# The middle column of a binary depthwise convolution taken from TensorE to DVE and ACT, and the input turned in later slices

## The chip, the cores and the metric

The kernel runs on one core of one Trainium2 chip. The metric is the device time of one execution in microseconds; the time before is the median of three runs.

## The reference

The input x has 16 images of 56 x 56 pixels and 384 channels, float32. Two layers follow each other, each added to its input:

```
x = x + attention(gn(x))       # dilated 3 x 3 attention, three groups of 128 channels, dilations 1, 2, 3
x = x + conv(gn(x), sign(w))   # depthwise 3 x 3 convolution, taps are -1, 0 or 1, zero padding
```

`gn` takes mean and variance over 12 channels and all pixels of an image and gives (g - m) / sqrt(s + eps), so for each image and channel it is a scale and a bias. In the second layer every channel has nine taps of its own. Of these, the taps with kx = 1 (the middle kernel column: the pixel above, the pixel itself, the pixel below) are what the change moves.

## The kernel before

The work is cut into 112 chunks: 16 images of 7 chunks, each of 8 rows (448 pixels). Channels lie on the partitions, in three groups of 128. The program is planned by hand in slices: a piece of work is put into a slice and an order within it with `at(when, order, piece)`, a chunk starts every 9 slices (`STEP`), and the pieces are emitted in the order of the slices. The framework then orders the instructions of each engine; each engine works its own queue in that order.

`plan_a` loads a chunk of x and turns it (TensorE transposes into PSUM, ACT copies to `xa`, DVE takes `bn_stats`, and SP's queue stores it channel-major as `xd`). In the kernel before the three groups are turned in slices 0, 2 and 4 of the chunk, for all images but the first. `plan_b` is the attention: products for q, k and v on TensorE (L464), scores as products q x k on DVE (L517) summed on TensorE (`ps`, L502), the softmax, then for each of nine groups of three neighbours the weights are spread over the partitions by TensorE into `pb_a` (L581), multiplied by v on DVE (`w`, L588) and added on GpSimd (L596); at last the output projection `po` (L614), its residual add on DVE (L617) and the store of the layer's result as `x1d`.

`plan_c` is the convolution. For channel groups 0 and 1, `load` brings x1 with the three rows of taps on 96 partitions (3 x 32 channels, one copy a kernel row) into `z`; `normalise` applies scale and bias on ACT (L698); `convolve` multiplies by diagonal weights `kdiag` on TensorE, four sets of 32 channels side by side, three kernel columns into one PSUM tile `pc` (L712); DVE adds the layer's input `x1` (L719). The third group (`zg`, `taps_g`, `sum_g`) is done by ACT and GpSimd without TensorE. `turn` transposes the result back and stores it. For the last image, whose convolution can only run after all other work, `z_last`, `taps_last` on DVE and other buffers are used.

PSUM tiles of many kinds (`pkv`, `po`, `pt_x`, `pt_o`, `pt_s`, `pc`) share the pool `ps_mt` with three banks; `pq` has one buffer, `pb_a` one.

Of the kernel before, what the change touches and what calls it, by code (L numbers as in the profile page):

```python
# [17 lines left out]
P = 128  # L18
# [17 lines left out]
def dilated_attention_then_binary_conv(  # L36
# [99 lines left out]

    spread = const.tile([P, 2, P], BF16, name="spread")

    ktap = const.tile([P, NTAP], F32, name="ktap")

    kdiag = const.tile([K3, 3, JG * NQ, HD], F32, name="kdiag")

    xin_p = ctx.enter_context(tc.tile_pool(name="xin_p", bufs=1))
    z_p = ctx.enter_context(tc.tile_pool(name="z_p", bufs=2))
    xa_p = ctx.enter_context(tc.tile_pool(name="xa_p", bufs=3))
    st_p = ctx.enter_context(tc.tile_pool(name="st_p", bufs=2))
    dr_p = ctx.enter_context(tc.tile_pool(name="dr_p", bufs=3, space=DRAM))
    xn_p = ctx.enter_context(tc.tile_pool(name="xn_p", bufs=3))
# [6 lines left out]
    x1_p = ctx.enter_context(tc.tile_pool(name="x1_p", bufs=2))  # L155
    xg_p = ctx.enter_context(tc.tile_pool(name="xg_p", bufs=2))
    m_p = ctx.enter_context(tc.tile_pool(name="m_p", bufs=3))
    o_p = ctx.enter_context(tc.tile_pool(name="o_p", bufs=2))


# [34 lines left out]
    def load_small_weights():  # L195

        raw["small"] = t = m_p.tile([P, 3, PX], F32, tag="m", name="small")
        flat = t.rearrange("p k n -> p (k n)")
        at_ = [0]

        def room(parts, n):
            at_[0] += n
            return flat[:parts, at_[0] - n : at_[0]]

        raw["b"] = room(NG, P)
        raw["k"], raw["kp"] = room(K3, 3 * NG * NQ), room(K3, 3 * NG * NQ)
        raw["kg"] = room(P, NTAP)
# [4 lines left out]
        nc.sync.dma_start(raw["kg"], w_conv.rearrange("y x c m -> c (y x m)")[JG * P : (JG + 1) * P, :])  # L212

    def load_taps(ky, kx):
        k_in = raw["k"].rearrange("p (k s) -> p k s", k=3)
# [17 lines left out]
    def small_weights():  # L233
        pt = ps_mt.tile([P, 512], F32, tag="mt", name="pt_b")
        nc.tensor.transpose(pt[:, :NG], raw["b"], ident[:NG, :NG])
        nc.vector.tensor_copy(bias, pt[:, :NG])

        spread_f = raw["spread"].rearrange("r (f n) -> r f n", f=2)
        nc.gpsimd.memset(spread_f, 0.0)
        for rg in range(4):  # L240
            for f in range(2):
                for t in range(TERMS):
                    halves = spread_f[:, f].rearrange("r (h d) -> r h d", h=HEADS)
                    nc.gpsimd.affine_select(
                        out=halves, in_=halves, compare_op=ALU.not_equal, fill=1.0,
                        base=-(32 * rg + (2 * t + f) * HEADS),
                        pattern=[[-1, HEADS], [0, HD]], channel_multiplier=1,
                    )
# [12 lines left out]

        binary(raw["kp"], raw["k"])
        kp = raw["kp"].rearrange("p (k s) -> p k s", k=3)
        binary(ktap, raw["kg"])
# [7 lines left out]
        for kx in range(3):  # L272
            nc.vector.tensor_tensor(
                kdiag[:, kx],
                kp[:, kx, : JG * NQ].unsqueeze(2).to_broadcast([K3, JG * NQ, HD]),
                eye3.unsqueeze(1).to_broadcast([K3, JG * NQ, HD]),
                ALU.mult,
            )
        raw.clear()

    def rows(ap):
        return ap.rearrange("p (r w) -> p r w", w=W)
# [113 lines left out]
    stats0, stats1 = {}, {}  # L396
    xd, x1d = {}, {}
    mr0, mr1 = {}, {}
    first = {}
    last_term = {}  # L400

    def plan_a(m, t0):
# [36 lines left out]
            elif j == NG - 1:  # L439
                nc.scalar.dma_start(chunk_of(xd[b], c), first[c])  # L440

        at(t0 - 3 if b else FIRST + 2 * max(c - 2, 0), LOADS, load)
        for j in range(NG):
            at(t0 + 2 * j if b else FIRST + 2 * c + 1, STAGE_A, lambda j=j: turn(j))

    def plan_b(m, t0):

# [197 lines left out]
        for j in range(NG):  # L645
            at(t0 + 24 + j, PROJECT, lambda j=j: out_project(j))

    def plan_c(m, t0):

        b, c = divmod(m, NCH)  # L650
# [38 lines left out]
        def normalise(j):  # L689
# [9 lines left out]
            for edge in edges(j):  # L699
                nc.gpsimd.memset(edge, 0.0)  # L700

        def load_x():
            had["x1"] = x1 = x1_p.tile([P, JG, PX], F32, tag="x1", name="x1")
            nc.sync.dma_start(x1, chunk_of(x1d[b], c)[:, :JG])  # L704

        def convolve(j):
            pc = ps_mt.tile([P, 512], F32, tag="mt", name="pc")
            pcr = rows(pc[:, :PX])

            def tap(kx, q):  # L710
                lo, hi = max(0, 1 - kx), W - max(0, kx - 1)
                return nc.tensor.matmul(  # L712
                    pcr[q * HD : (q + 1) * HD, :, lo:hi], kdiag[:, kx, j * NQ + q, :],
                    rows(set_of(j, q))[:, :, lo + kx - 1 : hi + kx - 1], start=(kx == 1), stop=(kx == 2),
                )
# [3 lines left out]
            nc.vector.tensor_tensor(x1[:, j], pc[:, :PX], x1[:, j], ALU.add)  # L719

        lo, hi = (0 if c else 1), ROWS + (2 if c < NCH - 1 else 1)
        zp = zg[m % 2]

        def load_g():
# [21 lines left out]
        def taps_last(ky):  # L746

            mid = had["xg"][:, 1 : ROWS + 1, :]
            if ky == 0:
                had["m"] = m_p.tile([P, 3, PX], F32, tag="m", name="m")  # L750
            acc = rows(had["m"][:, 0])
            for kx in range(3):
                o = 3 * ky + kx
                nc.vector.scalar_tensor_tensor(  # L754
                    mid if o == 8 else acc, zp[:, ky : ky + ROWS, kx : kx + W], ktap[:, o : o + 1],
                    acc if o else mid, op0=ALU.mult, op1=ALU.add,
                )

# [7 lines left out]
        def taps_g(ky):  # L766
            t = m_p.tile([P, 3, PX], F32, tag="m", name="m")
            for kx in range(3):
                o = 3 * ky + kx
                nc.scalar.activation(  # L770
                    rows(t[:, kx]), zp[:, ky : ky + ROWS, kx : kx + W], AF.Copy, scale=ktap[:, o : o + 1]
                )
            if ky == 0:
                had["m"] = t
# [13 lines left out]
        def turn(s):  # L788
            pt = ps_mt.tile([P, 512], F32, tag="mt", name="pt_o")
            mid = had["xg"][:, 1 : ROWS + 1, :].rearrange("p r w -> p (r w)")  # L790
            for j in range(NG):
                src = mid if j == JG else had["x1"][:, j]
                nc.tensor.transpose(pt[:SUB, j * P : (j + 1) * P], src[:, s * SUB : (s + 1) * SUB], ident)  # L793
            if b < B - 1:
                osb = o_p.tile([SUB, C], F32, tag="osb", name="osb")
# [7 lines left out]
        if b == B - 1:  # L803
# [54 lines left out]
    def statistics(when, sets):  # L858
# [60 lines left out]
```

## Time and profile before

| | before |
|---|---|
| median of 3 runs | 5223.8 us (5223.65 to 5231.6) |
| the profiled execution's own time | 5223.35 us |
| its span | 5221.6 us |
| PE busy | 5085.7 us |
| DVE busy | 4199.0 us |
| POOL busy | 4242.2 us |
| ACT busy | 2310.7 us |
| mean DMA rate | 158 GB/s |
| mean granted TensorE clock | 0.984 |

The busy times are those of one profiled execution, the span is from its first to its last instruction. PE is TensorE's matmul, PEld its weight load, DVE VectorE, ACT ScalarE, POOL GpSimd, SP the engine whose queue issues most of the DMAs. A share of busy time is a mean over stages with different limits.

### The profile page before, as it was taken

To read this page: it belongs to the slowest core of one execution; us is meant where nothing else is said; L and a number is where in the kernel's file an instruction comes from. 1 tells how busy PE (TensorE), PEld (TensorE's weight loads), DVE (VectorE), ACT (ScalarE), POOL (GpSimd) and SP (SyncE) were. 2 spreads that over 40 slices of the span, in tenths; PEclk is the share of its full clock that TensorE was granted. 3 is DMA by queue.
4 is the path that set the end of the run, shared out by engine and by line. 5 is a ranking of instruction groups with operands and counts; after the bars stand their busy time and mean duration, and the time that the engine had idled before them with its cause. 6 is when DMAs were issued, how large, how long until landed. Compare 5 with 4: busy or idle time off the path is not lost. (4 is left out here: it accounts for less than half of the span.)

```text
span 5221.6 us, 75614 instructions
## 1 busy us (share of the span) xinstructions
PE 5085.7 (97%) x26885; PEld 2322.5 (44%) x26885; DVE 4199.0 (80%) x4125; ACT 2310.7 (44%) x4077; POOL 4242.2 (81%) x2950
## 2 busy tenths in 40 slices
PE   8999999999999999999999999999999999999976
PEld 4444444444444444444444444444444444444433
DVE  4898888888888888888888888888888888878764
ACT  3223444444444544444444444444445444444444
POOL 2677878888888888889888888888888888888881
PEclk8999999999999999999999999999999999999987
DMA  6444656666566565656666565665666656554445
GB/s 197 127 124 119 167 160 166 163 166 167 162 169 165 161 163 159 168 158 166 166 166 165 163 166 162 165 163 160 164 163 171 167 163 168 141 138 135 121 135 158
DMA packets 811631, 825.62 MB, mean 158 GB/s; under 512 B 360307, under 2 KB 801014, under 8 KB 811254
## 3 DMA queue, kind: packets, MB, share of 16 engines
q1 hardware_dynamic: 803270, 808.79, 56.9%
q10 hardware_dynamic: 7984, 12.00, 0.7%
q8 instruction: 213, 3.49, 0.3%
q14 instruction: 164, 1.34, 0.1%
HBM read 466.41 MB, written 231.21 MB: 134 GB/s over the span
## 5 line engine op out<-in xcount | busy, mean ns | idle before, releaser
L596 POOL TENSOR_TENSOR w<-w 128x1344 f32<-128x1344 f32 x672 | 2048.7, 3049 | 327.3 <-DVE w L588 279.1
L517 DVE TENSOR_TENSOR t<-pq,k 128x1344 f32<-128x1344 f32 x1008 | 1528.6, 1550 | 237.8 <-PE pq L464 236.6
L588 DVE TENSOR_TENSOR w<-pb_a,v 128x1344 f32<-128x1344 f32 x1008 | 1560.3, 1548 | 172.6 <-PE pb_a L581 91.9
L464 PE MATMUL pkv<-xn,wqkvT 128*128 128x448 f32 x3924 | 1542.2, 542 | 3.9 <-ACT xa L435 3.5
L464 PEld LDWEIGHTS pkv<-xn,wqkvT 128*128 128x128 f32 x3924 | 725.9, 190 | 664.7 <-issue 634.7
L614 PE MATMUL po<-y,wprojT 128*128 128x448 f32 x2016 | 834.9, 550 | 17.3 <-POOL y L600 17.3
L464 PE MATMUL pq<-xn,wqkvT 128*128 128x448 f32 x1962 | 834.9, 560 | 0.0
L698 ACT ACTIVATE z<-z,mrz 96x448 f32<-96x448 f32 x840 | 573.9, 751 | 266.0 <-DMA z<-x1d 239.7
L777 POOL TENSOR_TENSOR m<-m 128x1344 f32<-128x1344 f32 x210 | 639.1, 3044 | 43.3 <-ACT m L770 37.9
L502 PE MATMUL ps<-t,sel 128*32 128x448 f32 x6048 | 660.8, 546 | 0.3 <-DVE t L517 0.2
L474 ACT COPY v<-pkv 128x448 f32<-128x448 f32 x336 | 178.1, 530 | 918.3 <-PE pkv L464 911.1
L770 ACT ACTIVATE m<-zg,ktap 128x448 f32<-128x448 f32 x945 | 552.6, 658 | 15.1 <-POOL m L777 5.7
L614 PEld LDWEIGHTS po<-y,wprojT 128*128 128x128 f32 x2016 | 376.1, 191 | 374.1 <-issue 347.1
L712 PE MATMUL pc<-z,kdiag 96*32 96x440 f32 (+1 forms) x5040 | 519.3, 545 | 7.1 <-POOL z L700 4.3
L464 PEld LDWEIGHTS pq<-xn,wqkvT 128*128 128x128 f32 x1962 | 345.2, 190 | 318.8 <-issue 318.8
L617 DVE SCALAR_TENSOR_TENSOR xr<-po,bias,xr 128x448 f32<-128x448 f32 x336 | 227.9, 678 | 277.8 <-PE po L614 272.7
L435 ACT COPY xa<-pt_x 128x448 f32<-128x448 f32 x315 | 167.4, 534 | 618.2 <-PE pt_x L423 618.2
L558 POOL TENSOR_TENSOR rest<-ew,e 112x512 f32<-112x512 f32 x112 | 130.1, 1162 | 358.9 <-ACT e L554 358.9
L581 PE MATMUL pb_a<-aT,spread 24*128 24x448 bf16 x3024 | 369.5, 360 | 42.7 <-DVE w L588 36.7
L600 POOL TENSOR_TENSOR y<-y,w 128x448 f32<-128x448 f32 x336 | 381.7, 1136 | 23.8
L599 POOL TENSOR_TENSOR y<-w 128x448 f32<-128x448 f32 x336 | 382.8, 1139 | 19.3
L581 PEld LDWEIGHTS <-spread 24*128 24x128 bf16 x3024 | 100.8, 91 | 621.4 <-issue 603.6
(132 smaller groups left out, 4307.6 us busy)
## 6 DMA issues: line engine op xcount, KB each, us to landing
z<-x1d SPq DMA_DIRECT2D x570, 224.0 KB, 4.0
xr<-xd SPq DMA_DIRECT2D x112, 672.0 KB, 4.3
x1d<-xr SPq DMA_DIRECT2D x112, 672.0 KB, 3.2
xn<-xd SPq DMA_DIRECT2D x109, 672.0 KB, 4.5
xin<-in_x_dram SPq DMA_DIRECT2D x105, 672.0 KB, 7.3
xd<-xa SPq DMA_DIRECT2D x315, 224.0 KB, 3.2
out_dram<-osb SPq DMA_DIRECT2D x420, 168.0 KB, 3.4
x<-x1d SPq DMA_DIRECT2D x112, 448.0 KB, 8.5
```

Of the source, the lines that this page charges most:

```text
L464: nc.tensor.matmul(dst[:, :PX], wqkvT[:, cc, o0 : o0 + P], had["xn"][:, cc, :], start=(cc == 0), stop=(cc == NG - 1))
L502: return nc.tensor.matmul(had["ps"][32 * j : 32 * j + 32, :PX], sel[:, s0 : s0 + 32], tk, start=(issued[j] == 1), stop=(issued[j] == len(r ...
L517: nc.vector.tensor_tensor(t.rearrange("p k (r w) -> p k r w", w=W), q3, k3, ALU.mult)
L581: return nc.tensor.matmul(pb[:, kx, :PX].rearrange("p (s n) -> p s n", s=NSUB), spread[rows_of, v % 2, :], had["a"][rows_of, :, v // 8, :] ...
L588: nc.vector.tensor_tensor(w.rearrange("p k (r w) -> p k r w", w=W), pb[:, :, :PX].rearrange("p k (r w) -> p k r w", w=W), three(kv[1][g][m ...
L596: nc.gpsimd.tensor_tensor(w0, w0, w, ALU.add)
L599: nc.gpsimd.tensor_tensor(y, w0[:, 0], w0[:, 1], ALU.add)
L614: nc.tensor.matmul(po[:, :PX], wprojT[:, g, j * P : (j + 1) * P], had[f"y{g}"], start=(g == 0), stop=(g == NG - 1))
L698: nc.scalar.activation(z, z, AF.Identity, bias=mrz[:, j, q, 0:1], scale=mrz[:, j, q, 1:2])
L712: return nc.tensor.matmul(pcr[q * HD : (q + 1) * HD, :, lo:hi], kdiag[:, kx, j * NQ + q, :], rows(set_of(j, q))[:, :, lo + kx - 1 : hi + k ...
L770: nc.scalar.activation(rows(t[:, kx]), zp[:, ky : ky + ROWS, kx : kx + W], AF.Copy, scale=ktap[:, o : o + 1])
L777: nc.gpsimd.tensor_tensor(had["m"], had["m"], t, ALU.add)
```

## The change

The middle kernel column leaves TensorE. Since the normalised input is scale x x1 + bias, the three middle taps of a pixel are a sum of three multiples of x1 and a constant. `column_scalars` computes the six numbers of each channel once an image on GpSimd. `column(j)` lets ACT compute the pixel's own tap, the layer's input and the constant into a new tile `u` (one buffer). `convolve(j)` keeps two columns on TensorE (8 matmuls in place of 12) and lets DVE add the tap above and the tap below with two `scalar_tensor_tensor`, which read and write `pc` in PSUM, and then `u`. For that x1 is loaded with a row above and one below (560 columns in place of 448), three slices earlier except in the last image. `ktap` holds all groups. To make room, `xa` has two buffers in place of three, `kdiag` loses a third, and the softmax's `sm` shares a buffer with `mx`. The pool of the third group's products (`m`) has three buffers in both kernels. The second part: x is turned in slices 3, 4 and 7 of a chunk, in place of 0, 2 and 4, and its load moves from slice -3 to slice 0.

```diff
-    ktap = const.tile([P, NTAP], F32, name="ktap")
+    ktap = const.tile([P, NG, NTAP], F32, name="ktap")
+    kcol = const.tile([P, JG, 3], F32, name="kcol")
-    kdiag = const.tile([K3, 3, JG * NQ, HD], F32, name="kdiag")
+    kdiag = const.tile([K3, 2, JG * NQ, HD], F32, name="kdiag")
-    xa_p = ctx.enter_context(tc.tile_pool(name="xa_p", bufs=3))
+    xa_p = ctx.enter_context(tc.tile_pool(name="xa_p", bufs=2))
+    u_p = ctx.enter_context(tc.tile_pool(name="u_p", bufs=1))
...
+        up, mid, down = (ktap[:, :JG, o] for o in (1, 4, 7))
+        nc.vector.tensor_add(kcol[:, :, 0], mid, down)
+        nc.vector.tensor_add(kcol[:, :, 1], kcol[:, :, 0], up)
+        nc.vector.tensor_add(kcol[:, :, 2], up, mid)
...
-        at(t0 - 3 if b else FIRST + 2 * max(c - 2, 0), LOADS, load)
+        at(t0 if b else FIRST + 2 * max(c - 2, 0), LOADS, load)
-            at(t0 + 2 * j if b else FIRST + 2 * c + 1, STAGE_A, lambda j=j: turn(j))
+            at(t0 + TURN_SLICE[j] if b else FIRST + 2 * c + 1, STAGE_A, lambda j=j: turn(j))
...
-            sm = s_p.tile([SUB, NSUB, GH], F32, tag="sm", name="sm")
+            sm = s_p.tile([SUB, NSUB, GH], F32, tag="mx", name="sm")
...
+    def column_scalars(b):
+        mr = mr1[b][0]
+        cs = st_p.tile([P, JG, 6], F32, tag="cs", name="cs")
+        nc.gpsimd.tensor_tensor(
+            cs[:, :, 0:3], ktap[:, :JG, 1:NTAP:3], mr[:, :JG, 1:2].to_broadcast([P, JG, 3]), ALU.mult
+        )
+        nc.gpsimd.tensor_tensor(cs[:, :, 3:6], kcol, mr[:, :JG, 0:1].to_broadcast([P, JG, 3]), ALU.mult)
+        nc.gpsimd.tensor_scalar(cs[:, :, 1], cs[:, :, 1], 1.0, None, op0=ALU.add)
+        cs1[b] = cs
...
         def load_x():
-            had["x1"] = x1 = x1_p.tile([P, JG, PX], F32, tag="x1", name="x1")
-            nc.sync.dma_start(x1, chunk_of(x1d[b], c)[:, :JG])
+            had["x1"] = x1 = x1_p.tile([P, JG, ROWS + 2, W], F32, tag="x1", name="x1")
+            nc.sync.dma_start(
+                x1[:, :, lo:hi, :].rearrange("p j r w -> p j (r w)"),
+                x1d[b].rearrange("(j p) n -> p j n", p=P)[:, :JG, p0 + (lo - 1) * W : p0 + (hi - 1) * W],
+            )
+
+        def column(j):
+            x1, cs = had["x1"], cs1[b]
+            had["u"] = u = u_p.tile([P, ROWS, W], F32, tag="u", name="u")
+            parts = [(0, 1, 3), (1, ROWS, 4)] if c == 0 else [(0, ROWS, 4)]
+            if c == NCH - 1:
+                parts = [(0, ROWS - 1, 4), (ROWS - 1, ROWS, 5)]
+            for r0, r1, of in parts:
+                nc.scalar.activation(
+                    u[:, r0:r1], x1[:, j, r0 + 1 : r1 + 1], AF.Identity, bias=cs[:, j, of : of + 1], scale=cs[:, j, 1:2]
+                )
...
-            in_one_go([lambda kx=kx, q=q: tap(kx, q) for kx in (1, 0, 2) for q in (3, 0, 1, 2)])
-            x1 = had["x1"]
-            nc.vector.tensor_tensor(x1[:, j], pc[:, :PX], x1[:, j], ALU.add)
+            in_one_go([lambda kx=kx, q=q: tap(kx, q) for kx in (0, 2) for q in (3, 0, 1, 2)])
+            x1 = had["x1"][:, j]
+            mid = x1[:, 1 : ROWS + 1]
+            cs, above, below = cs1[b], 1 if c == 0 else 0, ROWS - 1 if c == NCH - 1 else ROWS
+            nc.vector.scalar_tensor_tensor(
+                pcr[:, above:], x1[:, above:ROWS], cs[:, j, 0:1], pcr[:, above:], op0=ALU.mult, op1=ALU.add
+            )
+            nc.vector.scalar_tensor_tensor(
+                pcr[:, :below], x1[:, 2 : below + 2], cs[:, j, 2:3], pcr[:, :below], op0=ALU.mult, op1=ALU.add
+            )
+            nc.vector.tensor_tensor(mid, pcr, had["u"], ALU.add)
...
+                at(t0 + 1 + j, CONVOLVE, lambda j=j: column(j))
                 at(t0 + 1 + j, CONVOLVE, lambda j=j: convolve(j))
...
-        at(t0 - 1, LOADS, load_x)
+        at(t0 - 4, LOADS, load_x)
         for j in range(JG):
             at(t0 - 4 + 3 * j, LOADS, lambda j=j: load(j))
+            at(t0 + 2 + 3 * j + late, STATISTICS, lambda j=j: column(j))
...
+    TURN_SLICE = (3, 4, 7)
...
-                    (stats1[b], lambda mr, mrz, b=b: mr1.update({b: (mr, mrz)}), True) if layer
+                    (stats1[b], lambda mr, mrz, b=b: (mr1.update({b: (mr, mrz)}), column_scalars(b)), True) if layer
-        statistics(start_a(NCH * b + NCH - 1) + 5, [(0, b)])
+        statistics(start_a(NCH * b + NCH - 1) + (TURN_SLICE[NG - 1] + 1 if b else 5), [(0, b)])
```

More of the change, by code (lines that the diff above doesn't have):

```diff
@@ L206, in load_small_weights @@
         raw["k"], raw["kp"] = room(K3, 3 * NG * NQ), room(K3, 3 * NG * NQ)
-        raw["kg"] = room(P, NTAP)
+        raw["kg"] = room(P, NG * NTAP)
         raw["eye"] = room(K3, HD)
@@ L211, in load_small_weights @@
         nc.sync.dma_start(raw["b"], b_proj.rearrange("(j p) -> j p", p=P))
-        nc.sync.dma_start(raw["kg"], w_conv.rearrange("y x c m -> c (y x m)")[JG * P : (JG + 1) * P, :])
+        for j in range(NG):
+            nc.sync.dma_start(
+                raw["kg"][:, j * NTAP : (j + 1) * NTAP],
+                w_conv.rearrange("y x c m -> c (y x m)")[j * P : (j + 1) * P, :],
+            )
     def load_taps(ky, kx):
@@ L263, in small_weights @@
         kp = raw["kp"].rearrange("p (k s) -> p k s", k=3)
-        binary(ktap, raw["kg"])
+        binary(ktap.rearrange("p j o -> p (j o)"), raw["kg"])
+        up, mid, down = (ktap[:, :JG, o] for o in (1, 4, 7))
+        nc.vector.tensor_add(kcol[:, :, 0], mid, down)
+        nc.vector.tensor_add(kcol[:, :, 1], kcol[:, :, 0], up)
+        nc.vector.tensor_add(kcol[:, :, 2], up, mid)
         eye3 = raw["eye"]
@@ L271, in small_weights @@
             )
-        for kx in range(3):
+        for kx in (0, 2):
             nc.vector.tensor_tensor(
-                kdiag[:, kx],
+                kdiag[:, kx // 2],
                 kp[:, kx, : JG * NQ].unsqueeze(2).to_broadcast([K3, JG * NQ, HD]),
@@ L398, in dilated_attention_then_binary_conv @@
     mr0, mr1 = {}, {}
+    cs1 = {}
     first = {}
@@ L700, in normalise @@
                 nc.gpsimd.memset(edge, 0.0)
+        lo, hi = (0 if c else 1), ROWS + (2 if c < NCH - 1 else 1)
         def load_x():
-            had["x1"] = x1 = x1_p.tile([P, JG, PX], F32, tag="x1", name="x1")
-            nc.sync.dma_start(x1, chunk_of(x1d[b], c)[:, :JG])
+            had["x1"] = x1 = x1_p.tile([P, JG, ROWS + 2, W], F32, tag="x1", name="x1")
+            nc.sync.dma_start(
+                x1[:, :, lo:hi, :].rearrange("p j r w -> p j (r w)"),
[11 more added lines that the diff above has]
+                )
         def convolve(j):
@@ L710, in tap @@
             def tap(kx, q):
-                lo, hi = max(0, 1 - kx), W - max(0, kx - 1)
+                x0, x1 = max(0, 1 - kx), W - max(0, kx - 1)
                 return nc.tensor.matmul(
-                    pcr[q * HD : (q + 1) * HD, :, lo:hi], kdiag[:, kx, j * NQ + q, :],
-                    rows(set_of(j, q))[:, :, lo + kx - 1 : hi + kx - 1], start=(kx == 1), stop=(kx == 2),
-                )
-            in_one_go([lambda kx=kx, q=q: tap(kx, q) for kx in (1, 0, 2) for q in (3, 0, 1, 2)])
-            x1 = had["x1"]
-            nc.vector.tensor_tensor(x1[:, j], pc[:, :PX], x1[:, j], ALU.add)
-        lo, hi = (0 if c else 1), ROWS + (2 if c < NCH - 1 else 1)
+                    pcr[q * HD : (q + 1) * HD, :, x0:x1], kdiag[:, kx // 2, j * NQ + q, :],
+                    rows(set_of(j, q))[:, :, x0 + kx - 1 : x1 + kx - 1], start=(kx == 0), stop=(kx == 2),
+                    skip_group_check=True,
+                )
+            in_one_go([lambda kx=kx, q=q: tap(kx, q) for kx in (0, 2) for q in (3, 0, 1, 2)])
[7 more added lines that the diff above has]
+                pcr[:, :below], x1[:, 2 : below + 2], cs[:, j, 2:3], pcr[:, :below], op0=ALU.mult, op1=ALU.add
+            )
+            nc.vector.tensor_tensor(mid, pcr, had["u"], ALU.add)
         zp = zg[m % 2]
@@ L754, in taps_last @@
                 nc.vector.scalar_tensor_tensor(
-                    mid if o == 8 else acc, zp[:, ky : ky + ROWS, kx : kx + W], ktap[:, o : o + 1],
+                    mid if o == 8 else acc, zp[:, ky : ky + ROWS, kx : kx + W], ktap[:, JG, o : o + 1],
                     acc if o else mid, op0=ALU.mult, op1=ALU.add,
@@ L770, in taps_g @@
                 nc.scalar.activation(
-                    rows(t[:, kx]), zp[:, ky : ky + ROWS, kx : kx + W], AF.Copy, scale=ktap[:, o : o + 1]
+                    rows(t[:, kx]), zp[:, ky : ky + ROWS, kx : kx + W], AF.Copy, scale=ktap[:, JG, o : o + 1]
                 )
@@ L791, in turn @@
             for j in range(NG):
-                src = mid if j == JG else had["x1"][:, j]
+                src = mid if j == JG else had["x1"][:, j, 1 : ROWS + 1].rearrange("p r w -> p (r w)")
                 nc.tensor.transpose(pt[:SUB, j * P : (j + 1) * P], src[:, s * SUB : (s + 1) * SUB], ident)
```

## The prediction

> **What bounds the kernel now.** I read the share of each engine first, then the busy time in the steady stretch, then the waits of that stretch, then the groups of the lines that the change touches, last the end of the chain of waits. First the page's shares and slices:
>
> ```profile
> PE 5085.7 (97%) x26885; PEld 2322.5 (44%) x26885; DVE 4199.0 (80%) x4125; ACT 2310.7 (44%) x4077; POOL 4242.2 (81%) x2950
> ...
> PE   8999999999999999999999999999999999999976
> PEclk8999999999999999999999999999999999999987
> ```
>
> TensorE is busy from the second slice to the last but two, at full clock. The busy time of the window 1200 to 4500 us (PE, PEld, DVE, ACT, POOL, then clock, DMA share and GB/s):
>
> ```profile
> 1200.00:4500.00 3300.00, 3282.05 (x17532) 1497.50 (x17529) 2719.01 (x2637) 1542.38 (x2723) 2813.20 (x1856) 1.00 0.60 164
> ```
>
> TensorE's waits in that window (us, times, longest):
>
> ```profile
> PE pb_a L581 <- DVE w L588: 15.0, 11, 1.4
> PE pkv L464 <- ACT xa L435: 2.9, 10, 0.3
> ```
>
> TensorE is idle for 18 us of 3300. A busy TensorE may hide time that isn't matmul, but here its instructions follow each other with no wait, so a matmul removed moves all that follow. L588 has 9 instructions in a chunk and 80 in 400 us: a chunk takes 45.0 us, of which TensorE 44.8, DVE 37.1, POOL 38.4, ACT 21.0 (window / 3300 x 45). DVE's spare time is mostly waiting for TensorE's products (waits of the same window):
>
> ```profile
> DVE xr L617 <- PE po L614: 188.2, 84, 3.1
> ...
> DVE t L517 <- PE pq L464: 151.6, 211, 2.5
> DVE x L719 <- PE pc L712: 147.5, 116, 2.0
> ```
>
> The groups with shapes kept apart (count | busy us, mean ns):
>
> ```profile
> L712 PE MATMUL pc<-z,kdiag 96*32 96x440 f32 x3360 | 355.3, 541 | 0.0
> L712 PE MATMUL pc<-z,kdiag 96*32 96x448 f32 x1680 | 202.7, 554 | 7.1 <-POOL z L700 4.3 <-ACT z L698 2.5 <-DVE x L719 0.3
> L719 DVE TENSOR_TENSOR x<-pc,x 128x448 f32<-128x448 f32 x224 | 139.4, 622 | 241.6 <-PE pc L712 239.3 <-DMA x<-x1d 2.3
> L617 DVE SCALAR_TENSOR_TENSOR xr<-po,bias,xr 128x448 f32<-128x448 f32 x336 | 227.9, 678 | 277.8 <-PE po L614 272.7
> L698 ACT ACTIVATE z<-z,mrz 96x448 f32<-96x448 f32 x840 | 573.9, 751 | 266.0 <-DMA z<-x1d 239.7 <-issue 26.2
> ```
>
> The 448-wide form is the middle column, 1680 records of 5040. Four matmuls of 32 columns run side by side, which is why 5040 x 545 ns fill only 519.3 us (the page's L712).
>
> **What the Trainium skill says.** TensorEngine Tiling (Array Packing), Key Properties: tiles work independently and in parallel; the trace agrees (519.3 us, not 2747), so a removed column is worth a quarter of its records' sum. VectorE: DVE Perf Modes, Why PSUM operands drop a tier: fp32 with a PSUM operand runs at 1x; the trace agrees (L617 and L719, 448 elements in 678 and 622 ns). ScalarE: Activation LUTs, What ACT_TABLE_LOAD costs: 280 ns + 0.833 ns an element with one pointer operand, 93 ns for each more; for 448 and two pointers an estimate of 746, and L698 has 751. Perfetto Trace Analysis, Tensor Engine Instruction: ACT, DVE and GpSimd are strict FIFO; so what stands behind a waiting instruction waits too, as ACT's 239.7 us before L698 do for z's transfer.
>
> **The change, part by part.**
> 1. Removed: the tap kx = 1, a third of L712's records. 519.3 / 3 = 173 us for the 105 chunks of the first 15 images, 1.65 us a chunk. It counts where TensorE has no gaps: from the first convolution (about 430 us) to 5000 us, (5000 - 430) / 45 = 101 chunks: **-167 us**.
> 2. Added on DVE: two SCALAR_TENSOR_TENSOR over pc and x1 in each convolve, written into PSUM. Nearest row L617: 678 ns; it writes SBUF, so for a PSUM target I bound it by L719's 622 and by 800 and take 678. 4 x 0.68 = 2.7 us a chunk. The last add stays an L719 (622). DVE becomes 37.1 + 2.7 = 39.8 us of a chunk that TensorE could now do in 43.1: 92%. Not on TensorE's path as long as DVE's products come in time. I laid the new order of instructions of a steady chunk beside the durations above. TensorE asks DVE for w before each pb_a (one buffer), for t before each ps, and before the second pkv behind a convolve for that convolve's bank (three in ps_mt, now held 1.36 us longer). By this the bank has about 4 us, but two pb_a have near nothing: the second one of a chunk, which now stands ahead of the convolution instead of behind it, and the fifth, whose w stands on DVE behind the bn_stats of an x that is now turned just before. The first STT itself waits in DVE's queue for pc, and the third w stands behind it, with the next pb_a behind that. Per chunk I take 0.4 us of new waits (bounds 0.1 and 1.0): **+40 us** (10 to 100).
> 3. Added on ACT: u = scale x x1 + bias, two a chunk of 0.75 us (L698): 21.0 to 22.5 of 43. u_p has one buffer, so each waits for the last add of the convolve before, and behind it in ACT's queue stand the k and v copies, which give TensorE its banks. By the order the wait ends some 1.5 to 2.5 us before the copies are due: 0. If DVE is later than that, every later us is TensorE's.
> 4. The x1 load: 560 rather than 448 columns, 12.5 MB more on 826 (DMA share 0.60, so room), three slices sooner on SP's queue, right behind xg. Its 8.5 us to land in the page come with xin's 672 KB just ahead of it, which now comes later. u needs it; xg ahead of it lands in 3.6 us and ACT works 2.6 us on it, so up to 1.5 us of ACT wait, covered as in 3: 0. Buffer x1 of two chunks before has been turned out by then.
> 5. x turned in slices 3, 4, 7, its load three slices later and its xd stores likewise: the same instructions; each store still precedes its xn load by about nine chunks. xa's two buffers: the copy waits for the store two back, 3.2 us to land and about half a chunk old. The third bn_stats still stands ahead of the image's statistics. 0, but it is what decides the cushions in 2. POOL gets three small instructions an image (0.2 us each): under 10 us in all, in its slack of 4.7 us a chunk (43.1 - 38.4): 0. Weights: two more small loads and a few tiny DVE operations at the start: 0 to 2 us.
> 6. The last image's seven chunks, where TensorE isn't full. The end of the chain of waits, one chunk:
>
> ```profile
> 5191.20 5.01 DMA xg_last<-x1d
> 5196.29 0.82 ACT zg L741
> 5197.14 0.70 DVE m L754
> 5197.85 0.70 DVE m L754
> ...
> 5203.97 0.51 DVE z_last L694
> 5204.53 0.07 issue
> 5204.59 0.19 POOL z_last L700
> 5204.83 7.97 PE pc L712 x48
> 5212.81 0.48 PE pt_o L793 x3
> ```
>
> A chunk is 8 us of pc (at a granted clock of 0.73) and 5.5 us of add, turn and copy. The 8 becomes 5.3, but after the second pc the order has two STTs, two taps (0.70 each) and the add before the turn can start: 3.4 instead of 0.6 us; u adds 0.75 on ACT. -2.7 + 2.8 + 0.75 = about +0.9 a chunk: **+6 us** (-10 to +15).
>
> Sum against the profiled execution (5223.35 us, span 5221.6; the median of the runs is 5223.8): 5223.4 - 167 + 40 + 6 = **5102 us**; I say 5104 for the start. With the bounds 5060 to 5175.
>
> **The rivals.**
> *DVE sets the pace.* For it: 92%, and its queue waits for TensorE in an order of its own; of the 7.9 us that it idles now in a chunk, 5.2 would be left of a 45 us chunk. If 4.5 of these can't go, a chunk takes 39.8 + 4.5 = 44.3: 0.7 saved, 101 x 0.7 = 71, so 5223 - 71 + 6 = 5158; if all 5.2 stay, about 5225. Against: most of these waits are for products that come sooner when TensorE is faster.
> *Slower: the ring pc, DVE, ACT, bank.* Late STTs hold back u; u holds back the k and v copies in ACT's queue; these hold back TensorE's banks, and with them the next pc. The price is the two STTs of each convolve, paid by TensorE: 2 x 1.36 - 1.65 = +1.1 us a chunk, 5223 + 108 + 6 = 5337. It decides from 0.83 us of exposed wait per convolve. Against it the cushions of 1.5 to 4 us read from the order.
> *It doesn't do what it says.* The order has 8 matmuls in place of 12 for each convolve, so the work is gone; only its worth is open. If a column costs less than a third because the first one carries the start, 160 rather than 173 us: within the range.
>
> **How the numbers follow.** A change of 0.2% (10 us) is what a measurement of this kernel can tell from none. TensorE keeps the pace with small waits: 0.72, 5104, own range 5060 to 5175. DVE sets the pace: 0.16, 5155 to 5230. The ring: 0.10. Parts cancel near zero: 0.02. The range 5055 to 5190 leaves out the ring and the upper part of the DVE case. Faster: 0.72 + 0.12 = 0.84; within 0.2%: 0.05; slower: 0.11.
>
> **What would show it.** Right: L712 has 3360 records and about 350 us; a chunk (9 of L588) takes 43.3 to 43.9 us; TensorE's waits for DVE w grow to some 40 us, two or so a chunk at most; DVE 87 to 90% of the span; the last five chunks of the end 13 to 15 us apart. Wrong: PE's busy share falls to 95% or below in the steady stretch with waits for DVE w or t of over 1 us a chunk (first rival); or PE pkv and po waiting for ACT k and v, with ACT's u waiting for DVE's add (second). The STT's mean tells if PSUM as a target costs more.

## The result, and the profile after

The changed kernel takes 5216.2 us (median of 20 runs, 5201.0 to 5232.9), the kernel before beside it 5223.7 (20 runs, 5217.3 to 5231.6): ratio 0.9986, 95% interval 0.9976 to 0.9995, so a gain of 7.5 us. The profiled execution took 5203.25 us with a span of 5201.5. The forecast was 5104, range 5055 to 5190: **112 us too low, and outside the range**. Nearly all of the 167 us that the sum took off TensorE came back as something else.

Share of each engine in the page of after (engine, busy us, share of the span, instructions), and TensorE's slices:

```profile
PE 4974.5 (96%) x25093; PEld 2260.1 (43%) x25093; DVE 4499.2 (86%) x4575; ACT 2477.2 (48%) x4365; POOL 4241.8 (82%) x2998
...
PE   7999999999999999999999999999999999999975
```

DVE has its 300 us more, as forecast; TensorE has lost only 111. The busy time of the window 1200 to 4500 us (PE, PEld, DVE, ACT, POOL, clock, DMA share, GB/s):

```profile
1200.00:4500.00 3300.00, 3238.42 (x16512) 1472.63 (x16509) 2938.38 (x2953) 1660.87 (x2929) 2828.69 (x1897) 1.00 0.61 167
```

TensorE is now idle for 62 us of 3300 rather than 18. What it waited for there (us, times, longest), then two of GpSimd's waits of the same window, of which the second was 19.4 us before:

```profile
PE pb_a L593 <- DVE w L600: 37.0, 65, 2.0
PE po L626 <- ACT v L486: 12.3, 10, 2.7
PE pv L350 <- POOL dev L344: 6.4, 10, 1.3
```

```profile
POOL rest L570 <- ACT e L566: 134.4, 72, 4.6
POOL m L825 <- ACT m L818: 80.4, 55, 3.2
```

The groups of the lines that the change touches, shapes apart (count | busy us, mean ns | idle before):

```profile
L752 PE MATMUL pc<-z,kdiag 96*32 96x440 f32 x3360 | 363.4, 551 | 8.7 <-POOL z L723 7.5 <-ACT z L721 0.7 <-ACT osb L846 0.5
...
L762 DVE SCALAR_TENSOR_TENSOR pc<-x,cs,pc 128x448 f32<-128x448 f32 x192 | 131.8, 686 | 67.9 <-PE pc L752 44.5 <-issue 15.4 <-ACT u L742 2.7
...
L765 DVE SCALAR_TENSOR_TENSOR pc<-x,cs,pc 128x448 f32<-128x448 f32 x192 | 131.7, 687 | 5.1
...
L742 ACT ACTIVATE u<-x,cs 128x448 f32<-128x448 f32 x160 | 121.3, 758 | 38.3 <-DMA x<-x1d 26.5 <-DVE x L768 10.4 <-DVE t L529 0.7
```

The removed records are gone, and each new instruction costs what its nearest row said (686 ns against 678, 758 against 751). Prices were not the mistake.

A chunk (9 of L600) takes 44.59 us in this window, 44.93 before. Taken from the start of one matmul to the start of the next, `pc` went from 4.90 to 3.25 us a chunk, the 1.65 that I had forecast. All other groups together grew by 1.3 us: `ps` by 0.71, `pq` by 0.44, `pkv` by 0.16, `pb_a` by 0.11, `po` shrank by 0.12. The growth of `ps` is nearly all (0.60 us) one wait, that of the second `pb_a` of a chunk, which in most chunks (63 of 74) stands behind `ps` and asks for the w of the first.

Why is that w late? One chunk of after, in the timeline (start us, us, engine, line; only the lines of this chain, of GpSimd and of the second `pb_a`):

```profile
4046.48 3.05 POOL L608 TENSOR_TENSOR w<-w 128x1344 f32<-128x1344 f32 x1
...
4047.39 0.36 PE L593 MATMUL pb_a<-aT,spread 24*128 24x448 bf16 x3
...
4047.95 2.05 DVE L558 TENSOR_TENSOR ew<-ew,sm 112x432 f32<-112x432 f32 x1
...
4048.16 1.71 PE L514 MATMUL ps<-t,sel 128*32 128x448 f32 x16
...
4049.93 1.54 DVE L600 TENSOR_TENSOR w<-pb_a,v 128x1344 f32<-128x1344 f32 x1
...
4051.52 0.37 PE L593 MATMUL pb_a<-aT,spread 24*128 24x448 bf16 x3 [1.66 <-DVE w L600]
```

L558 is the softmax's normalising product. It takes 0.61 us elsewhere and 2.05 here, where GpSimd's addition L608 was running when it started and ended at 4049.53. The product ends 0.47 us after that. A GpSimd addition ran at its start in 41 of the 74 chunks of the window. In 39 of these the product ended 0.46 to 0.48 us after the addition; in the other two less than 0.05 us of the addition was left, and the product took its usual 0.61. So the longer time of the product is waiting for the addition (below I call this the lock). w stands behind it in DVE's queue, the second `pb_a` behind w, and all of TensorE behind that.

### The profile page after: what moved, and what is told of

It reads as the page before. It is cut to its first block, busy times and chain, and to the rows that moved or that the text cites. A ratio compares the mean times of both kernels' runs of the same rounds, so it can differ in the third digit from the quotient of the medians.

```text
span 5201.5 us, 72721 instructions
## 1 busy us (share of the span) xinstructions
PE 4974.5 (96%) x25093; PEld 2260.1 (43%) x25093; DVE 4499.2 (86%) x4575; ACT 2477.2 (48%) x4365; POOL 4241.8 (82%) x2998
## 3 DMA queue, kind: packets, MB, share of 16 engines
q8 instruction: 199, 3.26, 0.3%
## 5 line engine op out<-in xcount | busy, mean ns | idle before, releaser
L608 POOL TENSOR_TENSOR w<-w 128x1344 f32<-128x1344 f32 x672 | 2050.7, 3052 | 373.1 <-DVE w L600 346.1
L600 DVE TENSOR_TENSOR w<-pb_a,v 128x1344 f32<-128x1344 f32 x1008 | 1560.6, 1548 | 162.1 <-PE pb_a L593 101.5
L529 DVE TENSOR_TENSOR t<-pq,k 128x1344 f32<-128x1344 f32 x1008 | 1523.2, 1547 | 86.0 <-PE pq L476 75.8
L476 PE MATMUL pq<-xn,wqkvT 128*128 128x448 f32 x1962 | 893.2, 574 | 0.0
L818 ACT ACTIVATE m<-zg,ktap 128x448 f32<-128x448 f32 x945 | 572.1, 660 | 19.4 <-POOL m L825 10.3
L476 PEld LDWEIGHTS pq<-xn,wqkvT 128*128 128x128 f32 x1962 | 331.0, 190 | 390.1 <-issue 390.1
L846 ACT COPY osb<-pt_o 112x384 f32<-112x384 f32 x420 | 201.4, 480 | 508.9 <-PE pt_o L841 505.8
L629 DVE SCALAR_TENSOR_TENSOR xr<-po,bias,xr 128x448 f32<-128x448 f32 x336 | 227.5, 677 | 215.4 <-PE po L626 210.2
L593 PEld LDWEIGHTS <-spread 24*128 24x128 bf16 x3024 | 112.0, 91 | 616.2 <-issue 576.4
L752 PE MATMUL pc<-z,kdiag 96*32 96x440 f32 x3360 | 363.4, 551 | 8.7 <-POOL z L723 7.5
L486 ACT COPY k<-pkv 128x448 f32<-128x448 f32 x336 | 178.4, 531 | 362.6 <-PE pkv L476 362.5
```

The lines of the kernel that those rows point to most:

```text
L476: nc.tensor.matmul(dst[:, :PX], wqkvT[:, cc, o0 : o0 + P], had["xn"][:, cc, :], start=(cc == 0), stop=(cc == NG - 1))
L529: nc.vector.tensor_tensor(t.rearrange("p k (r w) -> p k r w", w=W), q3, k3, ALU.mult)
L593: return nc.tensor.matmul(pb[:, kx, :PX].rearrange("p (s n) -> p s n", s=NSUB), spread[rows_of, v % 2, :], had["a"][rows_of, :, v // 8, :] ...
L600: nc.vector.tensor_tensor(w.rearrange("p k (r w) -> p k r w", w=W), pb[:, :, :PX].rearrange("p k (r w) -> p k r w", w=W), three(kv[1][g][m ...
L608: nc.gpsimd.tensor_tensor(w0, w0, w, ALU.add)
L818: nc.scalar.activation(rows(t[:, kx]), zp[:, ky : ky + ROWS, kx : kx + W], AF.Copy, scale=ktap[:, JG, o : o + 1])
```

## The experiments

Times are medians in us; the kernel before, run beside them, gave 5221.8 to 5223.2. A `...` in a cut of code stands for what is left out. "An image" is the mean time of seven chunks over images 4 to 13 of the profiled execution: 314.3 before, 312.1 after.

**column_alone: the column moved, x turned as before**

```diff
-        at(t0 if b else ..., LOADS, load)
+        at(t0 - 3 if b else ..., LOADS, load)
-    TURN_SLICE = (3, 4, 7)
+    TURN_SLICE = (0, 2, 4)
```

> The middle column is off TensorE as in the changed kernel, but x is loaded and turned in slices 0, 2 and 4 as before. Theory A (the saving is spent on TensorE itself: the new slices put the second pb_a ahead of the convolution, where it waits for w, and let the first matmul of two or three queries a chunk stand apart from the other two): here only one query is split and the second pb_a stands behind the convolution, so most of the saving comes back: 5130 to 5180 us, chunks of about 43.5 us. Theory B (DVE's added 2.8 us a chunk set the pace, whatever the order): no better than the changed kernel, 5205 to 5230. Theory C (u behind DVE's add in ACT's queue holds the k and v copies): as B, with po and pkv waiting for ACT.

Measured 5146.8, ratio 0.9856 (0.9843 to 0.9869); an image 308.1. DVE and ACT do all the work that the changed kernel gives them, and it is 69 us faster. Theories B and C, as the main cause, don't survive it: with all of the added work most of the saving is there, so in the changed kernel it is the order of the work that costs.

**slices_alone: x turned later, three columns on TensorE**

```diff
 (in the kernel before)
-        at(t0 - 3 if b else ..., LOADS, load)
+        at(t0 if b else ..., LOADS, load)
-            at(t0 + 2 * j if b else ..., STAGE_A, ...)
+            at(t0 + (3, 4, 7)[j] if b else ..., STAGE_A, ...)
-        statistics(... + 5, [(0, b)])
+        statistics(... + (8 if b else 5), [(0, b)])
```

> The kernel before with x loaded and turned in slices 3, 4 and 7, its statistics three slices later; all three columns on TensorE and nothing added to DVE or ACT. Theory A: the slices alone cost 0.3 to 0.6 us a chunk by the second pb_a ahead of the convolution and by split queries: 5245 to 5285 us. Theory B: DVE has room here, so 5215 to 5232.

Measured 5301.8, ratio 1.0152 (1.0139 to 1.0165). The two parts of the change nearly cancel: the column alone is worth -76 us, the slices alone cost +79, and together they give -7.5. Theory A, though the time is 17 us above the range that I gave it.

**tap_left_out: the middle column gone, nothing added**

```diff
 (in the kernel before)
-            in_one_go([... for kx in (1, 0, 2) for q in (3, 0, 1, 2)])
+            in_one_go([... for kx in (0, 2) for q in (3, 0, 1, 2)])
```

> The kernel before with the middle column of the taps left out altogether (the convolution lacks it), so TensorE's saving alone with nothing added elsewhere. If the saving is worth its records and nothing else waits: 5224 - 167 = 5057, with one query split in two some 20 more: 5050 to 5085. Theory B' (DVE's or POOL's queue sets the pace even without added work): above 5130.

Measured 5082.4, ratio 0.9729 (0.9716 to 0.9742); an image 304.5, so a chunk loses 1.40 us and not 1.65. The column removed is worth 140 of the 167 us even with nothing in its place.

**no_stts: the changed kernel without the two additions on DVE**

```diff
-            nc.vector.scalar_tensor_tensor(pcr[:, above:], ...)
-            nc.vector.scalar_tensor_tensor(pcr[:, :below], ...)
```

> The changed kernel without its two SCALAR_TENSOR_TENSOR per convolve (the middle column's upper and lower taps are left out); u, the slices and TensorE's order stay. Theory A: the split queries stay (0.35 to 0.4 us a chunk, 40 us) and a part of the wait of the second pb_a: 5100 to 5150. Theory B (DVE's amount of work): all of the saving is there, 5055 to 5085. Theory C (u waits for DVE's add): 5150 to 5200, since u still waits for that add.

Measured 5234.3, ratio 1.0020 (1.0011 to 1.0029): **slower than with them**, which no theory had. TensorE's commonest order of a chunk is the same, DVE has 2.7 us a chunk less, and TensorE waits longer for w: 59.1 us of the window rather than 37.0. Its busy times of the window, then that wait:

```profile
1200.00:4500.00 3300.00, 3222.95 (x16334) 1462.23 (x16331) 2765.12 (x2620) 1650.71 (x2893) 2797.92 (x1878) 0.99 0.60 166
```

```profile
PE pb_a L593 <- DVE w L600: 59.1, 68, 3.1
```

The product L558 is part of it: its mean in the window is 1.33 us here, 1.02 in the changed kernel, 0.84 before. Whether it meets a running addition is a matter of when the two engines get there, not of how much either has to do. The other part is TensorE's clock, the 0.99 in the line above. In the window the trace has it at half for 11 stretches of 3.4 to 10.2 us, 65 us together, against 19 us in the changed kernel and 3.4 before. Beside each of the 11 lies an idle stretch of TensorE of 1.4 to 3.1 us. At half the clock half of such a time is lost, by my estimate up to 32 us here and 10 in the changed kernel. So long waits are paid for twice, and how the 18 us divide between the two was not tried.

**second_behind: the second `pb_a` of a chunk listed behind the convolution**

```diff
-            at(t0 + 14 + i - (pair == 1), WEIGH_AHEAD if pair == 0 else WEIGH, ...)
+            at(t0 + 14 + i - (pair == 1), WEIGH_AHEAD if pair == 0 and i != 6 else WEIGH, ...)
```

> The changed kernel with only the second pb_a of a chunk listed behind the convolution. The compiled order has then two queries whole that were split, and DVE's third w between the two SCALAR_TENSOR_TENSOR. Theory A1: 0.6 us of wait and 0.2 us of changes of group a chunk go: 5140 to 5170. If the wait only moves to the third or sixth pb_a, since DVE has the same work: 5195 to 5220.

Measured 5164.1, ratio 0.9890 (0.9877 to 0.9904); an image 309.6. The place is worth 52 us, together with what it brings with it: two queries of a chunk are whole that were split. But 0.32 us of wait is left at this `pb_a`, and L558 takes 1.85 us in the mean. This is the form of the answer that I had not expected: a convolution of cover, and the wait is still there.

**slices_second_behind: the same edit in slices_alone**

> The slices alone again, but the second pb_a of a chunk is listed behind the convolution, where the kernel before has it; all else as in slices_alone. Theory A1 (the price of the slices is the place of the second pb_a): its wait of 0.38 us a chunk and the changes of group around it go, 5301.8 to 5235 to 5265. Theory A2 (the price is elsewhere: the later statistics at the change of image, the turn of the third slice between po and pb_a): 5280 or more.

Measured 5268.7, ratio 1.0091 (1.0076 to 1.0107): 33 of the 79 us, less than A1 said. An image takes 316.9 against 314.3, and the first two images together 14 us more than before. In the window TensorE was at half its clock for 27 us, in the kernel before for 3.4, which by the estimate above is up to 12 us of the 46 that are left; the rest was not taken apart.

**no_u: no u on ACT**

```diff
-            nc.vector.tensor_tensor(mid, pcr, had["u"], ALU.add)
+            nc.vector.scalar_tensor_tensor(mid, mid, cs[:, j, 1:2], pcr, op0=ALU.mult, op1=ALU.add)
-            at(..., lambda j=j: column(j))
```

> The changed kernel without u on ACT: the last add of a convolve is a SCALAR_TENSOR_TENSOR of x1, its scale and pc (the constant part of the middle column is left out), the orders on TensorE and DVE stay. Theory C (u waiting in ACT's queue for DVE's add, and the products m, k and v behind it, cost the time): 5150 to 5185. Theory A: the same place of the second pb_a, so 5195 to 5225.

Measured 5187.5, ratio 0.9934 (0.9922 to 0.9946): 29 us, between the two theories. Of the 0.34 us a chunk that TensorE's groups gave back, 0.19 are in `ps`, ahead of the second `pb_a`, and 0.10 in `pkv`, behind which `po` waits for the v copies (12.3 us of the window before this edit, 7.2 after). So the k and v copies are the smaller part. GpSimd's wait for ACT's products m fell from 80.4 to 23.7 us in the window, GpSimd's w additions ran at the start of L558 in 18 chunks of 74 and not in 41, and L558's mean fell from 1.02 to 0.79 us. So my reading is that u pushes the products m back on ACT, these push GpSimd's additions, and they reach into L558. The three changes are measured; that they are one chain is not shown.

**column_psum: the softmax's sums in PSUM, on column_alone**

```diff
+    ps_one = ps_s.tile([P, 512], F32, name="ps")
-                had["ps"] = ps_s.tile([P, 512], F32, tag="s", name="ps")
+                had["ps"] = ps_one
-            sm = s_p.tile([SUB, NSUB, GH], F32, tag="mx", name="sm")
+            sm = ps_one[:SUB, PX : PX + NSUB * GH].rearrange("p (s k) -> p s k", s=NSUB)
```

> The column alone (column_alone), with the softmax's sums and their reciprocals in 48 spare columns of the score's PSUM bank, so that DVE's normalising multiplication has one operand in SBUF rather than two. It took 0.61 us where no GpSimd addition overlapped it and up to 2.4 where one did. Theory D (it waits for GpSimd's addition to end[...]): it takes 0.6 to 0.7 us in every chunk, the waits for w at the second pb_a (0.10 us a chunk) go, 5130 to 5142 us. If the long ones come from elsewhere, or a PSUM operand costs as much: 5143 to 5160.

Measured 5121.8, ratio 0.9810 (0.9796 to 0.9823). L558 takes 0.60 us in every one of 75 chunks, though a w addition overlaps it in 23 of them: theory D is right on the mechanism. The time fell by 25 us, more than I gave it (5130 to 5142), and not where I put it. An image went only from 308.1 to 307.9; 18 us came from the seven chunks after 98, where no more x is turned.

**second_psum: the sums in PSUM, on second_behind**

```diff
+            had["sm"] = pt[:SUB].rearrange("p (s v) -> p s v", s=NSUB)[:, :, NR : NR + GH]
-            sm = s_p.tile([SUB, NSUB, GH], F32, tag="mx", name="sm")
+            sm = had.pop("sm")
```

> second_behind with the softmax's sums in 48 spare columns of the PSUM tile of the turned scores, so that DVE's normalising multiplication has one SBUF operand; TensorE's order is that of second_behind. There this multiplication took 1.85 us in the mean (0.61 alone), and the second pb_a, which needs the w behind it, waited 0.32 us a chunk. Theory D (GpSimd's addition holds it up): 0.6 us in every chunk, the wait at the second pb_a gone: 5164 - 0.32 x 105 = 5130, range 5118 to 5140. If the wait is DVE's amount of work, it stays: 5155 to 5170.

Measured 5105.9, ratio 0.9774 (0.9760 to 0.9787); an image 305.3. The product in the view of its line (duration min/median/max in ns), first in second_behind, then here:

```profile
L558 DVE TENSOR_TENSOR ew<-ew,sm x112: 593/1914/3424, 107.5 to 4978.5; 112x432 f32<-112x432 f32 x112
```

```profile
L558 DVE TENSOR_TENSOR ew<-ew,pt_s x112: 590/603/606, 108.1 to 4915.0; 112x432 f32<-112x432 f32 x112
```

The longest is now less than a third of the old median, while GpSimd additions overlap the product in 65 chunks of 76. TensorE's waits of the window 1200 to 4500:

```profile
PE po L626 <- ACT v L486: 9.8, 10, 2.8
PE pb_a L593 <- DVE w L600: 6.6, 11, 2.4
PE pv L350 <- POOL dev L344: 4.5, 11, 0.7
```

The wait for w is down from 37.0 us in the changed kernel to 6.6 (23.6 in second_behind), and the time is 12 us below the range that I gave theory D. TensorE was at half its clock for 3.4 us of the window, in second_behind for 31, which by the estimate above is up to 14 us of the gain. That 5105.9 lies within 2 us of the 5104 of the prediction is chance: the prediction was for the changed kernel as it stands.

**ahead_psum: the sums in PSUM, the changed kernel's order held**

```diff
 (in second_psum, the second pb_a listed ahead again; for images 1 to 13)
+                with tc.issue_after(placed[m + 8, 6].ins) if j == 0 and ... :
                     ... the convolution's first matmul
+            with tc.issue_after(placed[m - 10, 0, 2, 2].ins) if g == 1 and ... :
                 project(pq, g * P)
```

> The changed kernel with the softmax's sums in PSUM (spare columns of the turned scores), and its own order on TensorE held by hand, the second pb_a ahead of the convolution, for images 1 to 13. If the GpSimd addition that holds up DVE's multiplication is what turned the place of the second pb_a from 0.25 into 0.60 us of wait a chunk: the multiplication takes 0.6 us always, the wait falls to 0.25 to 0.30 us, and the time to 5216 - 0.33 x 105 = 5181, range 5165 to 5190. If the two only count together (behind the convolution there is no wait left to save): below 5150. If the lock is not what makes w late: 5205 to 5220.

Measured 5135.1, ratio 0.9830 (0.9816 to 0.9843); an image 308.0, the second `pb_a` waits 0.16 us a chunk. This is more than I gave the lock alone (5165 to 5190), and in the branch below 5150, whose reason it does not bear out: behind the convolution there was a wait left to save. The order was held for 13 images only, so the images are the fair comparison (us an image, images 4 to 13). In each row of the table TensorE's commonest order of a chunk is the same in both kernels:

| | product waits for GpSimd | sums in PSUM |
|---|---|---|
| second `pb_a` ahead of the convolution | 312.1 (after) | 308.0 (ahead_psum) |
| second `pb_a` behind it | 309.6 (second_behind) | 305.3 (second_psum) |

The lock, with the loss of clock that its waits bring, costs 4.1 to 4.3 us an image, the place 2.5 to 2.7, and the two simply add.

**before_psum: the sums in PSUM, in the kernel before (the edit of column_psum)**

> The kernel before with the softmax's sums in spare columns of the score's PSUM bank, TensorE's order unchanged. There the multiplication is overlapped by a GpSimd addition in 13 chunks of 73 (0.84 us in the mean), and the second pb_a has 1.9 us to spare behind the convolution. If the lock was covered there: 5215 to 5224. If it cost as much as in the changed kernel: below 5195, and the change is not what exposed it.

Measured 5220.4, ratio 0.9998 (0.9989 to 1.0006); an image 314.8. The kernel before has the same lock (the product takes up to 3.36 us) and pays nothing for it. There the second `pb_a` stood behind a convolution of 12 matmuls and had 1.9 us to spare. The change did not create the lock; in the changed kernel the convolution no longer covers it. The 8 matmuls that are left can be cover enough: in column_alone they stand ahead of the second `pb_a`, and without the lock an image gained only 0.2 us. There the product ran beside a w addition in 29 chunks of 75, for 0.96 us in the mean. In second_behind, with the same 8 matmuls ahead, it was 63 of 74 and 1.85 us, and the cover was too short.

**column_whole_psum and second_whole_psum: queries kept together**

```diff
 (in column_psum and in second_psum)
-            project(pq, g * P)
+            in_one_go(list(project(pq, g * P)))
...
```

> column_psum with the nine matmuls of a query kept together, so that the sixth pb_a comes behind all of them instead of behind the first three. If a split query costs what I first held (some 0.15 us each by its extra changes of group): 5122 - 15 = 5107, range 5100 to 5113. If it costs nothing (the number of changes of group stays the same) and only the sixth pb_a's wait moves: 5114 to 5126.

> second_psum with the nine matmuls of each query kept together, so that the third query is no longer split by a pb_a. If a split has a price of its own (0.1 to 0.2 us a chunk): 5085 to 5098. If it only decides which pb_a waits: 5100 to 5112.

Measured 5104.1, ratio 0.9774 (0.9761 to 0.9788), a gain of 18 us; and 5163.0, ratio 0.9894 (0.9878 to 0.9910), a loss of 57. The same edit has opposite signs, so a split query has no fixed price, though the first time lies in the range that I gave to such a price. In the first, TensorE's wait for w falls from 12.6 to 0.4 us of the window. In the second, which lies outside both of my ranges, the compiled order puts the first w ahead of L558 on DVE in most chunks, and TensorE's waits for `po` on ACT's v rise from 9.8 to 25.1 us; that is all I can say of it.

**u_in_bank: u written into the convolution's bank ahead of the matmuls**

```diff
 (in column_whole_psum)
-            had["u"] = u = u_p.tile([P, ROWS, W], F32, tag="u", name="u")
+            had[f"pc{j}"] = pc = ps_mt.tile([P, 512], F32, tag="mt", name="pc")
+            u = rows(pc[:, :PX])
-                    ..., start=(kx == 0), stop=(kx == 2),
+                    ..., start=False, stop=(kx == 2),
...
```

> column_whole_psum with u written by ACT into the convolution's PSUM bank ahead of the matmuls, which then accumulate onto it; DVE has two instructions a convolve instead of three (1.25 us a chunk less) and the buffer of u is gone, so ACT's u no longer waits for DVE's add. Theory C (u's wait for DVE costs time through ACT's queue): the k, v and x copies come sooner, TensorE's 0.3 us a chunk of waits for ACT's xa go: 5075 to 5100. If a bank held longer by u is what is short: TensorE waits for ACT's u and time rises to 5120 or more. If TensorE alone is the bound: as column_whole_psum within 8 us.

Measured 5100.9, ratio 0.9769 (0.9756 to 0.9783), 3 us from column_whole_psum (this kernel does not compute the right convolution, so only its time is used). An image fell by 2.1 us, to 304.4, and the last 14 chunks lost 24 us of it again. In this order u's wait and 1.25 us of DVE work a chunk are together worth no more than 2.1 us an image: TensorE is the bound again.

**The version to keep.** second_psum (5105.9) and column_whole_psum (5104.1) are both 2.3% faster than the kernel before and 2.1% faster than the changed one. The first is the changed kernel with three lines edited.

## Why the prediction was wrong, point by point

**Step 1 (removal, -167) was right on TensorE's own account and a little high in its worth.** `pc` fell by 1.65 us a chunk as worked out; with nothing put in its place, tap_left_out gives 140 us.

**Step 2 (DVE, +40) is where the forecast failed, in the term "0.4 us of new waits" a chunk.** It named the right instruction, the second `pb_a`, "which now stands ahead of the convolution instead of behind it" (the fifth, which it named too, does not wait). It priced it wrongly, in two ways. First, I laid mean durations beside the order. The normalising product of the softmax stood there as one of many DVE rows, with a spread from 587 to 3362 ns that the view of its line in the kernel before shows and I did not ask for:

```profile
L546 DVE TENSOR_TENSOR ew<-ew,sm x112: 587/609/3362, 104.9 to 5035.8; 112x432 f32<-112x432 f32 x112
```

A median of 609 beside a maximum of 3362 is here a wait inside an instruction. The Trainium skill says what it is: SBUF — State Buffer, section "SBUF: two separate sides", has DVE and GpSimd share a pair of ports under an exclusive lock, and a DVE instruction with two SBUF inputs blocks against a GpSimd instruction that reads SBUF. The runs agree: with one of the two inputs in PSUM the product takes 0.60 us under the same additions. No row of the profile names it, since waits within an instruction are counted as its busy time and not among the waits. Second, I counted only waits. TensorE's other groups grew by 1.3 us a chunk in the changed kernel, of which idle time of TensorE is 0.6 (62 us against 18, over 74 chunks). The other 0.7 had no term in my sum: the half clock is up to 0.1 of it, the rest came with the new order and was not taken apart. In second_psum the growth is 0.47; the 0.85 between them are the lock and the place. That 0.47 is close to the 0.4 that I took only by chance, since TensorE's idle time there (21 us of 3300) has hardly grown.

**Step 3 (u, 0) was wrong by 29 us in the changed kernel**, as no_u shows. I followed u to the k and v copies behind it. By my reading of no_u it worked through the products m, GpSimd and the lock, so these 29 us are in part those of step 2 and do not add to them.

**Step 4 (the x1 load, 0)**: ACT waited for it before u for 30.2 us in the whole run, 0.3 us a chunk, where 1.5 was allowed, but once for 7.4 us. Nothing speaks against its 0; it was not tried apart. The whole kernel moved 10.8 MB more, not 12.5. **Step 5 (the slices, 0) was wrong by its method**: I checked each moved instruction for being in time, and the price lay in what the planner then put where they had been. Alone the slices cost 79 us; 33 of these are the place of the second `pb_a`. Yet with the lock off and the place mended, the kernel with the new slices (5105.9) is as fast as the best with the old ones (5104.1), so the slices have no fixed price. What makes up their other 46 us is open, but for the half clock. The first image also grew by 7 us (276.5 to 283.9); it takes 282.9 or more in every kernel with the new slices and 281.6 or less in every one with the old, and its cause was not tried. **Step 6 (the end, +6)**: from the last chunk's first w to the end 165.1 us against 170.5, so -5, inside its bounds but not by its sum: the last five chunks' turns come 13.3 to 13.7 us apart, as said, against 13.3 to 14.1 before, so the +0.9 a chunk did not come.

**The rivals.** "DVE sets the pace" had the size of the result about right (5155 to 5230) and the reason wrong: column_alone gives DVE all of that work and is at 5147, and no_stts takes it away and is slower; that its size fitted was chance. "The ring pc, DVE, ACT, bank" did not come; u_in_bank removes u's part of it in a good order for 2.1 us an image. Of my signs for being wrong, PE's busy share of the steady window (98.1%) and the waits for w (0.5 us a chunk) did not show the first rival, and the second showed weakly (`po` waited 12.3 us for v, u 58.5 us for DVE's add). Of those for being right, the waits for w came as said (37.0 us); the chunk's 44.6 us, where I had 43.3 to 43.9, showed that it was not.

## What to carry to other kernels

When cover is taken away from an instruction (here the convolution that stood ahead of a `pb_a`), look at the minimum, median and maximum of everything in its chain of inputs, not at the means: a long tail can be a wait that was hidden and will now be paid. An edit that moves pieces in a planner's list is to be read in the compiled order on every engine, and each part of a two-part change is to be run alone: -76 and +79 looked like "no change". A DVE product of two SBUF tiles beside a busy GpSimd can be worth an operand in PSUM, if a few columns of a bank are free: here 58 us (second_psum) where the product stood in TensorE's way, and nothing (before_psum) where it did not.

## What the runs showed of the hardware that I had not expected

- The lock is sharp: in 39 of the 41 chunks where a GpSimd addition ran at its start, the DVE product ended 0.46 to 0.48 us after that addition, for a product that takes 0.61 us alone. The longest of second_behind took 3.42 us, 2.8 more, a little less than one GpSimd addition (3.05). The one that starts first goes first: seven times in the first image of after an addition started 0.22 to 0.24 us after the product did, and there the product took 0.59 to 0.60 us and the addition 3.26 to 3.27.
- DVE's products of one PSUM and one SBUF tile (w at 1548 ns, t at 1547, the longest of 1008 each 1559) run beside the same additions at their usual time, and moving one operand to PSUM costs the product nothing (603 against 609 ns).
- Less work on an engine made the kernel slower: without 2.7 us of DVE work a chunk it takes 18 us more, while the product is held up longer by the additions (1.33 us in the mean, against 1.02).
- Half clock of TensorE for 3.4 to 10.2 us stands beside idle stretches of 1.4 to 3.1 us, 11 times in 3300 us of no_stts, so a wait can cost more than its length.
- SCALAR_TENSOR_TENSOR in place in PSUM takes 686 ns for 448 elements, 9 more than L629's 677, which has its target in SBUF and other operands too.
